# Layer 1 of a four-layer graph network: one joined product of turned h, and the splits, squares and bias moved around it

## The chip, the core and the metric

The kernel runs on one core of one Trainium2 chip. The time is device time in microseconds (us), the median of three runs. Engine names are those of the profile: PE (TensorE, matmuls; PEld are its weight loads), DVE (VectorE), ACT (ScalarE), POOL (GpSimd) and SP (SyncE, which here issues the DMAs). L12 means line 12 of the kernel.

## The reference, cut to what matters

x is 32 batches of 512 nodes with 128 features, adj is 512 x 512. Four graph layers follow each other; each adds its result to x. Layer 1 is the one that is changed:

```python
h = maximum(layernorm(x), 0)
x1 = einsum('bnf,nw->bwf', h, adj)             # first hop
x2 = 2 * einsum('bnf,nw->bwf', x1, adj) - h    # second hop
xs = stack([h, x1, x2, x1, x2])                # the two adjacencies of the layer are the same
x = x + relu(xs.reshape(b, n, 5 * 128) @ Theta1 + bias)
```

With Theta1 in five blocks of 128 rows, the kernel forms T0 = block 0 - (block 2 + block 4), T1 = block 1 + block 3 and T2 = 2 (block 2 + block 4), and computes `h T0 + adj^T (h T1 + x1 T2) + bias`: the own product h T0, the weighed product in the bracket, and one mix with adj for both hops. Layer 2 multiplies by the elementwise square of adj (`adj * adj`), which is why that square is prepared while layer 1 runs.

## The kernel before, in words

**Stages.** In the profiled execution layer 0 fills the time up to about 183 us, layer 1 runs from there to 450 us, layer 2 to about 645 us and layer 3 to the end. `tc.manual_schedule` makes PE, DVE, ACT and POOL run their instructions in the order in which the source writes them. SP's queue is ordered by the scheduler, except for DMAs under `keep_in_program_order`.

**Precision by parts.** Most large products run in F32R, a form of f32 that TensorE takes in one record, on three parts of each operand, `high`, `low` and `mid`: three F32R products accumulate into one PSUM bank. A product of plain f32 shows as two records. The parts of adj (`adj_parts`) are made once, at the end of layer 0. `moving_parts(x, high, low, mid)` splits a tile of 128 x 512: ACT writes high (L420), POOL low (L421), DVE mid (L422). `mixed_parts` is the product of such parts with `adj_parts`: twelve F32R matmuls with 512 columns (L405), and one ACT copy out (L407).

**Layer 1** works in rounds. A pair q holds two batches, b = 0 and 1; round r holds pairs A = 2r and C = 2r + 1, so there are 16 pairs and 8 rounds. For each pair:

- `normalised(q)`: eight ACT instructions make h (L285).
- `split_up(q, b)`: the three parts of h, node-major (`high_h`, `low_h`, `mid_h`).
- `turn(q)`: h turned to feature-major: two DVE transposes in blocks of 32 (L321), four DMA writes of the blocks to DRAM and one DMA load back as hT (L328, L330).
- `straighten(q)`: two POOL copies (L974) of hT into `hs`, in node order.
- `first(q, b)`: x1, feature-major, by `mixed_parts` of the parts of h.
- `weighed(q, b)`: for each of four blocks of 128 nodes, `hs T1 + x1 T2` as two plain f32 matmuls with 128 columns (L447), one PSUM bank in all; then w's three parts, high on ACT (L992), low and mid on DVE (L993, L994).

And for each round, `mix(r, i)` for the four node blocks i: first the own product `hs T0` as four plain f32 matmuls (L999), then twelve F32R matmuls of w's parts with `adj_parts` into the same bank (L1003), then two DVE passes: scale and bias (L1005), relu and the sum into x (L1007).

Round r writes its instructions so that the mixes of round r - 1 stand at its head: the PE order is mix(r-1, 0..3), first(A, 1), weighed(A, 0), weighed(A, 1), first(C, 0), first(C, 1), weighed(C, 0), weighed(C, 1), first(A+2, 0). Between them the source calls the splits, turns and normalisations of later pairs, `ln_stats` (layer norm statistics: four DVE instructions L245, a square root on ACT, two small DVE ones) for layer 2, and steps of `square`, the generator that makes the squared adjacency on POOL: it loads adj in crossed order, then for each of four blocks makes `sq_high` and `sq_low` in two steps (L1345 to L1349), and at the end `sq_mid` in four POOL instructions (L1354). `go(steps, n)` runs n steps of a generator. In the last round `more(k)` starts layer 2: its first h (`chunk`), their turning (`turn_half`, `fetch`) and the first two `features`. `messages(n)` is the first matmul group of layer 2: parts of the features with `sq_high`, `sq_low`, `sq_mid`.

**Buffers.** Tiles of 128 x 512 with the tag `small` (the parts of h, x1) share 13 buffers, the wide ones (parts of w and of the square) 6, `hT` and `hs` together 4, h 3. PSUM has 8 banks.

Of the kernel before, what the change touches and what calls it, by code (L numbers as in the profile page):

```python
# [9 lines left out]
F32 = mybir.dt.float32  # L10
# [19 lines left out]
def kernel(  # L30
# [369 lines left out]
    def mixed_parts(name, left, right, dst):  # L400
# [6 lines left out]
        nc.scalar.activation(dst, p, AF.Copy, scale=UP)  # L407
# [10 lines left out]
    def moving_parts(x, high, low, mid):  # L418

        nc.scalar.activation(high, x, AF.Copy, scale=DOWN)  # L420
        nc.gpsimd.tensor_sub(low, x, high.bitcast(F32))  # L421
        nc.vector.scalar_tensor_tensor(mid, x, 1.0 / UP, high.bitcast(F32), OP.mult, OP.subtract)  # L422

# [309 lines left out]
    def late_parts():  # L733
# [10 lines left out]
        nc.gpsimd.tensor_scalar(th[:, 0, :], th[:, 0, :], 1.0 / UP, None, OP.mult)  # L744
# [205 lines left out]
    def layer1(more, square):  # L950


        h, hT, hs, parts, x1, w = {}, {}, {}, {}, {}, {}
# [26 lines left out]

        def first(q, b):
# [4 lines left out]
        def weighed(q, b):  # L986
            r, j = q // 2, 2 * (q % 2) + b
            if j == 0:
                w[r] = [wide_tile(f"w_{part}_{r}", F32R) for part in PARTS]
            p = projected(f"p_w_{q}_{b}", (columns(hs[q][:, b]), th[:, 1, :]), (columns(x1[q, b]), th[:, 2, :]))  # L990
            high, low, mid = (part.rearrange("p t (w f) -> p t w f", f=D)[:, :, j, :] for part in w[r])
            nc.scalar.activation(high, p, AF.Copy, scale=DOWN)  # L992
            nc.vector.tensor_sub(low, p, high.bitcast(F32))  # L993
            nc.vector.scalar_tensor_tensor(mid, p, 1.0 / UP, high.bitcast(F32), OP.mult, OP.subtract)  # L994

        def mix(r, i):
            p = bank(f"p_l1_{r}_{i}")
            for j in range(4):
                nc.tensor.matmul(p[:, blk(j)], columns(hs[2 * r + j // 2][:, j % 2])(i), th[:, 0, :],  # L999
                                 start=(j == 0), stop=False, skip_group_check=True)  # L1000
            for part in range(3):
                for t in range(NT):
                    nc.tensor.matmul(p, adj_parts[part][:, t, blk(i)], w[r][part][:, t, :],  # L1003
                                     start=False, stop=(part == 2 and t == NT - 1), skip_group_check=True)
            nc.vector.scalar_tensor_tensor(tiles(p), tiles(p), UP, spread(b1, 4), OP.mult, OP.add)  # L1005
# [8 lines left out]
        split_up(0, 0)  # L1014
        split_up(0, 1)
        first(0, 0)
        straighten(0)
        turn(1)
        for r in range(NQ // 2):
            A, C = 2 * r, 2 * r + 1  # L1020
            last = r == NQ // 2 - 1
            if r == 0:
                first(A, 1)
                split_up(C, 0)
                split_up(C, 1)
                straighten(C)
            else:
# [5 lines left out]
                mix(r - 1, 1)  # L1033
                normalised(C)
                turn(C)
# [394 lines left out]
```

## Time and profile before

| | |
|---|---|
| median of 3 runs | 912.63 us (912.6 to 913.73) |
| profiled execution, own time | 912.96 us |
| its span, first to last instruction | 911.2 us |
| granted TensorE clock | 1.00 throughout |
| stretch of layer 1 in the trace | about 183.6 to 450.6 us |
| one round of layer 1 | 33.0 to 33.1 us |
| chain that ended last | PE 92%, ACT 3%, DVE 3%, POOL 1% |

The span is what the profile can be divided into; the own time of the same execution is 1.8 us longer, because it includes what lies before the first and after the last instruction. Busy shares on the page are means over four different layers, so a stage has to be read from its own stretch of the trace. Durations of matmul records overlap: two records of 275 ns can start 112 ns apart.

### The profile page before, as it was taken

How to read it: one execution, taken by the hardware profiler on the slowest of the kernel's cores; microseconds unless marked ns; L12 is line 12 of the kernel's file. 1: busy time of each engine (PE TensorE's matmuls, PEld its weight loads, DVE VectorE, ACT ScalarE, POOL GpSimd, SP SyncE). 2: the span in 40 equal slices, each digit the busy share in tenths (PEclk: the TensorE clock that was granted, in tenths of full speed). 3: DMA queues.
4: the chain of work that ended last, by engine and by line, in shares of the span. 5: the costliest groups of instructions: out<-in, count | busy, mean ns of one | idle time of the engine just before them, and what ended most of it. 6: DMA issues, size and time to landing. Idle time of an engine off the chain costs nothing.

```text
span 911.2 us, 15170 instructions
## 1 busy us (share of the span) xinstructions
PE 901.1 (99%) x5432; PEld 774.2 (85%) x5433; DVE 669.7 (74%) x1348; ACT 527.5 (58%) x1156; POOL 485.6 (53%) x435
## 2 busy tenths in 40 slices
PE   8999999999999999999999999999999999999998
PEld 4899999988888888888877777777789999999998
DVE  7888886566656665665767777777698888987775
ACT  5874554343532442452556768876577767666663
POOL 5867999932132163342254445545475555666553
PEclk9999999999999999999999999999999999999999
DMA  9255644123114313212332344455212223222111
GB/s 265 50 167 165 186 122 118 24 71 93 35 59 119 87 31 90 71 46 76 106 120 70 93 126 129 132 147 160 70 48 82 81 82 91 73 70 81 59 36 47
DMA packets 83915, 86.06 MB, mean 94 GB/s; under 512 B 6784, under 2 KB 74624, under 8 KB 83840
## 3 DMA queue, kind: packets, MB, share of 16 engines
q1 hardware_dynamic: 83552, 84.57, 32.8%
q8 instruction: 43, 0.70, 0.3%
q10 hardware_dynamic: 288, 0.52, 0.2%
q14 instruction: 32, 0.26, 0.1%
HBM read 44.17 MB, written 40.89 MB: 93 GB/s over the span
## 4 chain that ended last, share of the span: by engine, by line
PE 92%; ACT 3%; DVE 3%; POOL 1%; issue 0%; DMA 0%; DVEq 0%; POOLq 0%; ACTq 0%
PE p_av L1234 12%; PE p_l L1003 10%; PE p_x1T L405 9%; PE p_score L1212 9%; PE p_msgT L1142 9%; PE p_w L447 6%; PE p_l_c L393 4%; PE p_l L999 3%; PE p_l_a L393 3%; PE p_l_d L393 3%; PE p_g L447 3%; PE p_l L447 3%; PE p_hv L447 3%; PE p_feat L447 3%; PE p_phi L1151 3%; PE p_phi L1152 3%
## 5 line engine op out<-in xcount | busy, mean ns | idle before, releaser
L1234 PEld LDWEIGHTS p_av<-hv,ex 128*128 128x128 f32 x1024 | 119.3, 191 | 3.7 <-POOL ex L1207 1.0
L1234 PE MATMUL p_av<-hv,ex 128*128 128x129 f32 x1024 | 119.8, 274 | 0.8 <-POOL ex L1207 0.8
L421 POOL TENSOR_TENSOR low_feat<-feat,high_feat 128x512 fp32r<-128x512 f32 x32 | 53.9, 1686 | 115.8 <-ACT high_feat L420 111.7
L285 ACT ACTIVATE h<-x,sh,rs 128x128 f32<-128x128 f32 x256 | 102.8, 483 | 11.8 <-DVE sh L257 11.0
L1207 DVE TENSOR_TENSOR ex<-ex,adjTx 128x512 f32<-128x512 f32 x64 | 80.4, 1259 | 35.7 <-ACT ex L1205 34.0
L1207 POOL TENSOR_TENSOR ex<-ex,adjTx 128x512 f32<-128x512 f32 x64 | 98.1, 1551 | 12.2 <-ACT ex L1205 8.1
L1093 ACT ACTIVATE h<-x,sh,rs 128x128 f32<-128x128 f32 x256 | 102.9, 485 | 0.0
L428 POOL TENSOR_TENSOR key<-key 128x512 fp32r<-128x512 f32 x32 | 50.2, 1567 | 97.9 <-DVE key L427 39.8
L421 POOL TENSOR_TENSOR low_h<-h,high_h 128x512 fp32r<-128x512 f32 x32 | 47.1, 1482 | 76.6 <-ACT high_h L420 76.4
L245 DVE BATCH_NORM_STATS2 bn<-x 128x6 f32<-128x256 f32 x244 | 85.9, 417 | 0.0
L407 ACT ACTIVATE x1T<-p_x1T 128x512 f32<-128x512 f32 x32 | 19.0, 594 | 109.4 <-PE p_x1T L405 100.8
L1205 ACT ACTIVATE ex<-ex 128x512 f32<-128x512 f32 x128 | 78.9, 651 | 0.0
L1213 ACT ACTIVATE ex<-p_score 128x512 f32<-128x512 f32 x128 | 74.0, 604 | 1.4 <-PE p_score L1212 1.1
L974 POOL COPY hs<-hT 128x512 f32<-128x512 f32 x32 | 18.6, 612 | 81.5 <-DMA hT<-d_hT 81.3
L432 ACT ACTIVATE high_query<-p_query 128x512 fp32r<-128x512 f32 x32 | 19.2, 599 | 73.8 <-PE p_query L1185 73.8
L422 DVE SCALAR_TENSOR_TENSOR mid_feat<-feat,high_feat 128x512 fp32r<-128x512 f32 x32 | 28.9, 904 | 44.3 <-ACT high_feat L420 44.3
L1212 PE MATMUL p_score<-high_query,key 128*128 128x512 f32 x128 | 50.5, 394 | 0.0
L1212 PE MATMUL p_score<-low_query,key 128*128 128x512 f32 x128 | 50.3, 393 | 0.0
L1212 PE MATMUL p_score<-mid_query,key 128*128 128x512 f32 x128 | 50.3, 393 | 0.0
L447 PE MATMUL p_w<-th,x1T 128*128 128x128 f32 x256 | 49.6, 275 | 0.3 <-ACT x1T L407 0.3
L254 ACT ACTIVATE sd<-bn,eps 128x8 f32<-128x8 f32 x46 | 13.9, 302 | 61.5 <-DVE bn L245 57.4
L447 PE MATMUL p_w<-th,hs 128*128 128x128 f32 x256 | 49.4, 275 | 0.0
(220 smaller groups left out, 2350.4 us busy)
## 6 DMA issues: line engine op xcount, KB each, us to landing
d<-hb SPq DMA_DIRECT2D x128, 128.0 KB, 2.5
hT<-d SPq DMA_DIRECT2D x32, 512.0 KB, 3.4
d_hT<-hb_hT SPq DMA_DIRECT2D x112, 128.0 KB, 2.4
hT<-d_hT SPq DMA_DIRECT2D x28, 512.0 KB, 3.3
x<-in_x_dram SPq DMA_DIRECT2D x32, 256.0 KB, 5.0
out_dram<-x SPq DMA_DIRECT2D x31, 256.0 KB, 2.3
adjT_d<-adj_squares SPq DMA_DIRECT2D x4, 256.0 KB
adj_crossed<-in_adj_dram SPq DMA_DIRECT2D x4, 256.0 KB
```

The lines of the kernel that those rows point to most:

```text
L245: nc.vector.bn_stats(st[:, k].rearrange("p e s -> p (e s)"), xt[q][:, b, t : t + 2, :].rearrange("p t f -> p f t"))
L285: nc.scalar.activation(h[:, b, t, :], xt[q][:, b, t, :], AF.Relu, bias=shift[q][:, i : i + 1], scale=scale[q][:, i : i + 1])
L393: nc.tensor.matmul(p[:, i * 2 * D : (i + 1) * 2 * D], a[:, k, blk(i)], b[:, k], start=(first and i == 0 and k == 0), stop=(k == 1), skip_g ...
L405: nc.tensor.matmul(p, right[part][:, blk(t)], left[part][:, t, :], start=(t == 0 and part == 0), stop=(t == NT - 1 and part == 2))
L421: nc.gpsimd.tensor_sub(low, x, high.bitcast(F32))
L447: nc.tensor.matmul(p[:, blk(t)], hT(t), w, start=(i == 0), stop=(i == len(terms) - 1))
L1003: nc.tensor.matmul(p, adj_parts[part][:, t, blk(i)], w[r][part][:, t, :], start=False, stop=(part == 2 and t == NT - 1), skip_group_check= ...
L1093: nc.scalar.activation(h[:, t, :], xt[q][:, b, t, :], AF.Relu, bias=shift[q][:, i : i + 1], scale=scale[q][:, i : i + 1])
L1142: nc.tensor.matmul(p, feats[n][part][:, blk(t)], sq[part][:, t, :], start=(t == 0 and part == 0), stop=(t == NT - 1 and part == 2))
L1207: eng.tensor_mul(split(ex[:, t, :]), split(ex[:, t, :]), crossed(mask[:, t, :]))
L1212: nc.tensor.matmul(p, keys[n][i][:, t, :], query[n][i], start=(i == 0), stop=(i == 2))
L1234: nc.tensor.matmul(po[:, i, : D + 1], ex[:, t, blk(i0 + i)], hv[:, t, :], start=(t == 0), stop=(t == NT - 1))
```

## The change

- Turned h (`hs`) is split into three F32R parts as well (`split_turned`, new), and T0 and T1, which lie side by side in `th`, into three parts once (`fixed_parts`, new, 128 x 256).
- `weighed` multiplies the parts of turned h with T0 and T1 joined, 256 columns at once, so one product gives both the own product and the first term of the weighed one. x1 T2 stays a plain f32 matmul with 128 columns, added into the right half. A batch now fills two banks in place of one. Each bank is read by two ACT instructions (w's high part, and the own half, which is written over `hs`) and two DVE instructions (low, mid), each over half a bank.
- `biased_own` (new) adds the bias to the own half on POOL.
- `mix` loses its four f32 matmuls. Its first DVE pass becomes two half passes that add the own half; the second pass is unchanged.
- The factor `UP` moves from x1's copy and th into the evictions of `weighed`.
- The calls are written in a new order: at the entry three first products stand ahead of the first weighed one; in a round `split_up` of C moves behind the mixes and the new splits are spread between the products; `normalised` and `turn` of A + 2 move; the steps of `square` are called behind the third mix of rounds 3 to 6, two at a time; the statistics for layer 2 come two rounds later, and those of two more pairs fall into layer 2.

```diff
--- before.py
+++ after.py
@@ -404,7 +404,7 @@
             for t in range(NT):
                 nc.tensor.matmul(p, right[part][:, blk(t)], left[part][:, t, :],
                                  start=(t == 0 and part == 0), stop=(t == NT - 1 and part == 2))
-        nc.scalar.activation(dst, p, AF.Copy, scale=UP)
+        nc.scalar.copy(dst, p)
 
     def three(name):
         return [small_tile(f"{part}_{name}", F32R) for part in PARTS]
@@ -420,6 +420,13 @@
         nc.scalar.activation(high, x, AF.Copy, scale=DOWN)
         nc.gpsimd.tensor_sub(low, x, high.bitcast(F32))
         nc.vector.scalar_tensor_tensor(mid, x, 1.0 / UP, high.bitcast(F32), OP.mult, OP.subtract)
+
+    def fixed_parts(x, high, low, mid):
+
+        nc.scalar.activation(high, x, AF.Copy, scale=DOWN)
+        nc.gpsimd.tensor_sub(x, x, high.bitcast(F32))
+        nc.scalar.activation(low, x, AF.Copy, scale=LOW)
+        nc.gpsimd.tensor_sub(mid, high.bitcast(F32), low.bitcast(F32))
 
     def scaled_parts(x_low, high, low, mid):
 
@@ -741,7 +748,6 @@
         for out, op, p, q in ((1, OP.add, 1, 3), (2, OP.add, 2, 4), (0, OP.subtract, 0, 2)):
             tc.keep_in_program_order(nc.gpsimd.tensor_tensor(th[:, out, :], th[:, p, :], th[:, q, :], op))
         tc.keep_in_program_order(nc.gpsimd.tensor_scalar(th[:, 2, :], th[:, 2, :], 2.0, None, OP.mult))
-        nc.gpsimd.tensor_scalar(th[:, 0, :], th[:, 0, :], 1.0 / UP, None, OP.mult)
         for t in range(NT):
             nc.scalar.activation(low[:, t, :], adj_s[:, t, :], AF.Copy, scale=LOW)
         yield
@@ -950,7 +956,7 @@
     def layer1(more, square):
 
 
-        h, hT, hs, parts, x1, w = {}, {}, {}, {}, {}, {}
+        h, hT, hs, parts, hs_parts, x1, w = {}, {}, {}, {}, {}, {}, {}
         normal, turning = {}, {}
 
         def normalised(q, n=2 * NT):
@@ -978,31 +984,51 @@
                 parts[q, b] = three(f"h_{q}_{b}")
                 moving_parts(h[q][:, b].rearrange("p t f -> p (t f)"), *parts[q, b])
 
+        def split_turned(q, b):
+            hs_parts[q, b] = three(f"hs_{q}_{b}")
+            moving_parts(hs[q][:, b], *hs_parts[q, b])
+
         def first(q, b):
             if q < NQ:
                 x1[q, b] = small_tile(f"x1T_{q}_{b}")
                 mixed_parts(f"x1T_{q}_{b}", adj_parts, parts[q, b], x1[q, b])
 
         def weighed(q, b):
+
+
             r, j = q // 2, 2 * (q % 2) + b
             if j == 0:
                 w[r] = [wide_tile(f"w_{part}_{r}", F32R) for part in PARTS]
-            p = projected(f"p_w_{q}_{b}", (columns(hs[q][:, b]), th[:, 1, :]), (columns(x1[q, b]), th[:, 2, :]))
-            high, low, mid = (part.rearrange("p t (w f) -> p t w f", f=D)[:, :, j, :] for part in w[r])
-            nc.scalar.activation(high, p, AF.Copy, scale=DOWN)
-            nc.vector.tensor_sub(low, p, high.bitcast(F32))
-            nc.vector.scalar_tensor_tensor(mid, p, 1.0 / UP, high.bitcast(F32), OP.mult, OP.subtract)
+            ps = [bank(f"p_w_{q}_{b}_{i}") for i in range(2)]
+            for t in range(NT):
+                p = ps[t // 2][:, t % 2 * 2 * D : (t % 2 + 1) * 2 * D]
+                for part in range(3):
+                    nc.tensor.matmul(p, hs_parts[q, b][part][:, blk(t)], th_parts[part],
+                                     start=(part == 0 and t % 2 == 0), stop=False, skip_group_check=True)
+                nc.tensor.matmul(p[:, D:], x1[q, b][:, blk(t)], th[:, 2, :], start=False, stop=True,
+                                 skip_group_check=True)
+            for i, p in enumerate(ps):
+                p = p.rearrange("p (t k f) -> p k t f", t=2, k=2)
+                high, low, mid = (part.rearrange("p t (w f) -> p t w f", f=D)[:, 2 * i : 2 * i + 2, j, :]
+                                  for part in w[r])
+                nc.scalar.activation(high, p[:, 1], AF.Copy, scale=UP * DOWN)
+                nc.scalar.activation(tiles(hs[q][:, b])[:, 2 * i : 2 * i + 2, :], p[:, 0], AF.Copy, scale=UP)
+                nc.vector.scalar_tensor_tensor(low, p[:, 1], UP, high.bitcast(F32), OP.mult, OP.subtract)
+                nc.vector.tensor_sub(mid, p[:, 1], high.bitcast(F32))
+
+        def biased_own(q):
+            for b in range(2):
+                nc.gpsimd.tensor_add(tiles(hs[q][:, b]), tiles(hs[q][:, b]), spread(b1, NT))
 
         def mix(r, i):
             p = bank(f"p_l1_{r}_{i}")
-            for j in range(4):
-                nc.tensor.matmul(p[:, blk(j)], columns(hs[2 * r + j // 2][:, j % 2])(i), th[:, 0, :],
-                                 start=(j == 0), stop=False, skip_group_check=True)
             for part in range(3):
                 for t in range(NT):
                     nc.tensor.matmul(p, adj_parts[part][:, t, blk(i)], w[r][part][:, t, :],
-                                     start=False, stop=(part == 2 and t == NT - 1), skip_group_check=True)
-            nc.vector.scalar_tensor_tensor(tiles(p), tiles(p), UP, spread(b1, 4), OP.mult, OP.add)
+                                     start=(part == 0 and t == 0), stop=(part == 2 and t == NT - 1))
+            for k in range(2):
+                pk = tiles(p)[:, 2 * k : 2 * k + 2, :]
+                nc.vector.scalar_tensor_tensor(pk, pk, UP, hs[2 * r + k][:, :, blk(i)], OP.mult, OP.add)
             x = xq[r].rearrange("p w b t f -> p (w b) t f")[:, :, i, :]
             nc.vector.scalar_tensor_tensor(x, tiles(p), 0.0, x, OP.max, OP.add)
 
@@ -1011,64 +1037,75 @@
         turn(0)
         normalised(1)
         yield
-        split_up(0, 0)
-        split_up(0, 1)
+        for q, b in ((0, 0), (0, 1), (1, 0)):
+            split_up(q, b)
+        pair = small_tile("th_high", F32R), small_tile("th_low", F32R)
+        th_parts = pair[0][:, : 2 * D], pair[0][:, 2 * D :], pair[1][:, : 2 * D]
+        fixed_parts(th[:, 0:2, :].rearrange("p k f -> p (k f)"), *th_parts)
+        normalised(2)
+        straighten(0)
         first(0, 0)
-        straighten(0)
         turn(1)
+        split_turned(0, 0)
+        first(0, 1)
+        split_turned(0, 1)
+        first(1, 0)
+        straighten(1)
         for r in range(NQ // 2):
             A, C = 2 * r, 2 * r + 1
             last = r == NQ // 2 - 1
-            if r == 0:
-                first(A, 1)
-                split_up(C, 0)
-                split_up(C, 1)
-                straighten(C)
-            else:
+            early, late_stats = ((stats_steps(q) if r > 1 else iter(())) for q in (A - 4, C - 4))
+            if r:
                 split_up(A, 1)
                 straighten(A)
                 mix(r - 1, 0)
                 normalised(C, NT)
                 turn(C, 1)
                 mix(r - 1, 1)
+                go(early, NT)
                 normalised(C)
                 turn(C)
+                split_turned(A, 0)
                 mix(r - 1, 2)
+                split_turned(A, 1)
+                go(square, 2 * (2 < r < 7))
+                go(early, 1)
+                normalised(A + 2)
+                mix(r - 1, 3)
+                go(early)
+                first(A, 1)
                 split_up(C, 0)
-                go(square, r > 3)
-                mix(r - 1, 3)
-                split_up(C, 1)
-                first(A, 1)
+                straighten(C)
             weighed(A, 0)
+            split_up(C, 1)
             weighed(A, 1)
             if last:
                 more(0)
-            go(square, r > 2)
-            first(C, 0)
-            normalised(A + 2, NT)
+            split_turned(C, 0)
+            biased_own(A)
+            first(C, 0 if r else 1)
+            go(late_stats, NT)
             if last:
                 more(1)
+            split_turned(C, 1)
+            turn(A + 2, 1)
             if r:
-                ln_stats(A - 2)
-            else:
-                go(own[NQ - 3])
-                go(own[NQ - 2])
-            first(C, 1)
+                first(C, 1)
+            go(late_stats, 1)
             if last:
                 more(2)
-            if r:
-                straighten(C)
             split_up(A + 2, 0)
-            normalised(A + 2)
-            go(square, r > 3)
+            turn(A + 2)
             weighed(C, 0)
             weighed(C, 1)
-            ln_stats(C - 2) if r else go(own[NQ - 1])
-            go(square, r > 3)
-            turn(A + 2)
+            go(late_stats)
+            biased_own(C)
+            go(square, r == 2)
             first(A + 2, 0)
             if r == 0:
                 normalised(C + 2, 0)
+                for q in (NQ - 3, NQ - 2, NQ - 1):
+                    go(own[q])
         more(3)
         for i in range(NT):
             mix(r, i)
@@ -1287,8 +1324,8 @@
                 fetch(2, 2)
             elif n % 2 and n + 5 < B:
                 fetch(2, n // 2 + 3)
-            if n in (2, 3):
-                ln_stats(NQ - 4 + n)
+            if n in (2, 3, 4, 5):
+                ln_stats(NQ - 6 + n)
             if n == 12:
                 weights_of_3()
             if n == 20:
```

`fixed_parts`, `split_turned` and `biased_own` are new and stand in the diff in full; `moving_parts`, `stats_steps` and `bank` are not changed.

## The prediction

> **What bounds the kernel now.** I read the page's busy shares first, then the stage of layer 1 (179 to 451 us) by stretches, then who waited for whom on PE, and last the chain and single instructions.
>
> ```profile
> PE 901.1 (99%) x5432; PEld 774.2 (85%) x5433; DVE 669.7 (74%) x1348; ACT 527.5 (58%) x1156; POOL 485.6 (53%) x435
> ...
> 352.50:385.50 33.00, 33.00 (x194) 28.73 (x193) 20.09 (x36) 13.29 (x30) 15.43 (x17) 1.00 0.24 65
> ...
> PE p_w L447 <- ACT x1T L407: 0.3, 1, 0.3
> ```
>
> The second line is one round of layer 1 (columns: stretch, its length, busy PE, PEld, DVE, ACT, POOL, granted clock, DMA share, GB/s): PE has no free moment in 33 us, the next engine is at 61%. The last is PE's only wait in the whole layer. So a round lasts as long as its matmuls, and the change has to be priced by how far apart matmuls start. A record overlaps the next one, so spacing comes from the chain:
>
> ```profile
> 388.34 3.57 PE p_w L447 x32
> ...
> 404.71 2.80 PE p_l L1003 x12
> 408.40 2.81 PE p_l L1003 x12
> ```
>
> 32 records of weighed in 3.57 us: an f32 product with 128 columns is two records of 111.6 ns, 223 ns in all. Twelve F32R products with 512 columns take 2.80 us, 233 ns each. One mix follows the other by 3.69 us, so its eight records of L999 (the own product) take 0.89 us.
>
> **What the Trainium skill says.** "TensorE: Matmul & The Clock Gate", Back-to-back issue gap and LDWEIGHTS: warm matmuls start N/2.4 + 2.5 ns apart, 128 weight columns load in 107 ns. For 512 bf16 columns the trace agrees (six in 1.29 us, 216 ns); the F32R products lie 17 ns above it, and no page prices F32R. Its section on the clock gate: about 3.4 us without matmuls halve the clock. PE's longest wait here is 2.0 us and the clock is 1.00 throughout, so no trace shows that. "SBUF — State Buffer", two separate sides: VectorE with two SBUF inputs and GpSimd exclude each other from a shared port pair. In the tile views mid_h on DVE takes 681 to 1761 ns and low_h on POOL 1272 to 1803 ns, which fits; I use both ends.
>
> **The change, part by part.**
>
> 1. *The product on PE.* Per batch it removes 16 f32 records in weighed and 8 in mix: 24 x 111.6 = 2.68 us. It adds 12 F32R products with 256 columns and keeps 8 f32 records for x1T (0.89 us). No row has the 256-column form. Weights:
>
> ```profile
> 371.37 0.30 PEld L1003 LDWEIGHTS p_l<-w_high,adj_high 128*128 128x128 f32 x2
> L1003 PEld LDWEIGHTS p_l<-w_low,adj_low 128*128 128x128 f32 x128 | 24.1, 188 | 5.9
> ```
>
> Two F32R loads in 0.30 us, each 188 ns long: the second starts 0.11 us after the first, so a load allows 112 to 116 ns. Streaming: half of 233 is 116 ns; if the 17 ns are a fixed charge it is 126 ns. I take 121 ns: 12 x 121 + 893 = 2.35 us, a gain of 0.334 us per batch, 32 times **-10.7 us** (116 ns: -12.6; 126 ns: -8.8). Switches between f32 and F32R: a mix takes 3.696 us against 8 x 111.6 + 12 x 232.7 = 3.685, so about 5.5 ns each. Four more per batch: **+0.7**.
>
> 2. *What the other engines get, per round.* ACT: four high parts (0.60) and 16 evictions of half a bank (0.37, the ACT row L342) for four of 0.59: +5.9, 19.2 us. DVE: four mid parts at 0.98, 16 half evictions at 0.42 (DVE row L342) for eight at 0.69, half a pass more per mix: about +5.7, 25.8 us. POOL: four low parts at 1.48, four bias adds at 1.28 (as L841): +11, 19.4 us, 23 where it squares. A round of PE is then 31.8 us, so none becomes the bound by load.
>
> 3. *Order inside a round.* PE, from the first mix: mixes to 11.2; first(A,1) 14.0; weighed(A) 16.3 and 18.7; first(C) 21.5 and 24.3; weighed(C,0) 26.6; weighed(C,1) 29.0; first(A+2,0) 31.8. The new wait is weighed's for the parts of turned h. The tight one is (C,1): ACT splits (C,0) behind the last eviction of weighed(A,1), at 20.1; then POOL does low(C,0) 1.3, two bias adds 2.6, low(C,1) 1.3, done at 25.3, needed at 26.7. Slack 1.4 us. Turned h of C: transposed by 9.5, and at the entry the transposes' end (177.9) to the copy (186.1) takes 8.1, so it is there at 17.6; straighten and low_h(C,1) end at 20.1, just ahead of that chain. Behind it on POOL wait low_h(A+2,0) and bias C, both with over 2 us. SP keeps its instructions; each pair's four writes are now followed by its own load, while before some loads sat behind the other pair's write. The half-bank evictions use two banks a batch; sixteen banks a round are two turns of eight and each is read in time. Small tiles: 13, less two for th's parts; the count reaches 11 behind x1 of (A,1), and every later split stands in ACT's queue behind a copy that already waited for the release. Cost **+0.4**; ends 0 and 8.
>
> 4. *Entry.* Three first products (8.4 us) stand ahead of weighed(0,0). In that time POOL has low(1,0), two pieces of th (0.77 each, as L1169) and straighten(0) ahead of low(0,0); ACT has eight normalisations (3.1 us) ahead of high(0,0). Low(0,0) ends at 192.5 against 192.1. Later turned h of pair 1 lands near 196 and holds low_h(1,1): 0.7; in round 0 only one first product lies between weighed(0,1) and weighed(1,0), so low(1,1), behind two bias adds, is 1.0 late. 2.1 less the 0.3 there now: **+1.8**; ends 0 and 4.
>
> 5. *The square's mid part.* Two steps a round from rounds 3 to 6 complete high and low. The mid part falls to the call after layer 1, on POOL behind low_feat of batch 1; before, it was made at 387 us.
>
> ```profile
> L1354 POOL TENSOR_TENSOR sq_mid<-sq_high,sq_low x4: 1260/1273/1717, 387.4 to 391.6; 128x512 fp32r<-128x512 f32 x4
> ...
> 449.67 1.77 POOL L421 TENSOR_TENSOR low_feat<-feat,high_feat 128x512 fp32r<-128x512 f32 x1 [2.27 <-ACT high_feat L420]
> ...
> 450.74 2.77 PE p_msgT L1142 x12
> ```
>
> Counted from the end of the second mix, low_feat of batch 1 ends at 9.9 now and about 10.2 after (DVE's mix is a little longer); PE reaches messages(0) at 0.89 + 2.8 + 0.89 + 2.8 = 7.4, and its mid products at 9.2. The four pieces come at 11.5, 12.7, 14.0 and 15.2; PE ends at 15.5 for 10.2. **+5.3**; ends 3 and 8, the latter if the clock is halved for a while. What queues behind is messages(1) and features(2), whose parts are ready by then.
>
> 6. *At nothing.* Plain copies for scaled ones and th's scale dropped: same instructions, one POOL piece less, under layer 0's matmuls. Statistics of four pairs move from layer 1 into blocks 2 to 5 of layer 2, 1.8 us on DVE each; DVE has 1.8 us free in a block of 6.3 and blocks 2 and 3 carry it already. If that cover goes, 1 us. The last round's work for layer 2 lies on ACT ahead of high(C,1), inside the slack of 3.
>
> Sum: -10.7 + 0.7 + 0.4 + 1.8 + 5.3 = **-2.5 us**. The profiled execution took 912.96 us (span 911.2), 0.3 over the median of 912.63, so 910.5 there and 910.2 against the median. 0.2% is 1.8 us, what a measurement can tell from no change.
>
> **Rivals.**
>
> *The waits shrink (0.15).* The product at 116 ns and an entry without waits: -12.6 + 0.7 + 5.3 = -6.6, 906. For it: PE's present lack of any wait; against it: item 5's queue order, which is fixed.
>
> *POOL sets the round (0.25), slower.* The place is low(C,1) behind the bias adds. With low parts at 1.8 and adds at 1.5 the chain ends at 26.7 and the slack is gone; each further 0.1 us is lost in seven rounds. Being 1 us late costs 7 us: +4.5, 917; at 1.4 us 920. It decides from about 0.6 us. For it: low_feat's 1.77 us on a POOL that meets DVE; against it: low_h's median of 1304 ns.
>
> *256 columns give no gain (0.05), slower.* If the F32R product stays at 233 ns whatever its width, weighed takes 3.69 us a batch: +32 us, 942. The load spacing speaks against it. Outside my range.
>
> **Numbers.** Main case 0.55, its own range 906 to 914: of it 0.33 faster, 0.17 same, 0.05 slower. With the rivals: faster 0.49, same 0.21, slower 0.30. The range 903 to 918 takes in the cheap product with few waits and POOL about 1 us late a round.
>
> **What would show it.** Right: L1006 products 116 to 126 ns apart; rounds of about 32 us with PE full; a wait of PE for sq_mid near 5 us at the first messages. Wrong: weighed waiting for low_hs in every round; L1006 spaced by more than 149 ns, where item 1's gain is gone; no wait for sq_mid.

## The result and the profile after

The kernel after takes **920.34 us** (median of four runs, 920.09 to 921.09) against 912.82 before (912.60 to 913.73): 1.0082 of the time before, 95% interval 1.0064 to 1.0099. It is slower by 7.5 us where the prediction said 910.2, range 903 to 918. The profiled execution has a span of 918.5 us, 7.3 over the 911.2 before.

First the page's busy row, then PE's waits (engine, line, waited for: us in total, times, longest):

```profile
PE 897.3 (98%) x5304; PEld 765.6 (83%) x5305; DVE 709.0 (77%) x1476; ACT 569.4 (62%) x1286; POOL 583.8 (64%) x500
```

```profile
PE p_w L1006 <- POOL low_hs L421: 6.8, 5, 2.0
PE p_msgT L1179 <- POOL sq_mid L1391: 3.6, 4, 2.2
```

PE is recorded busy for 3.8 us less and still ends later. Before, its only wait in layer 1 was 0.3 us; now there are five stops of `weighed` for the low part of turned h, 6.8 us, and four at the first messages, 3.6 us. A view of stretches and a piece of the chain show that the product itself is as fast as hoped:

```profile
343.90:375.50 31.60, 31.60 (x178) 27.28 (x177) 25.66 (x52) 18.40 (x46) 24.33 (x20) 1.00 0.24 68
```

```profile
421.67 0.36 PE p_w L1006 x3
422.03 0.22 PE p_w L1008 x2
422.25 0.36 PE p_w L1006 x3
```

In an undisturbed round PE is full (31.60 of 31.60 us) and the round lasts 31.6 us where it lasted 33.05; three products with 256 columns take 0.36 us, 120 ns each. The next line of stretches is round 3 of the same kernel: 34.02 us long, PE busy 32.15.

```profile
278.18:312.20 34.02, 32.15 (x177) 27.29 (x177) 25.71 (x52) 18.61 (x46) 23.66 (x20) 1.00 0.33 101
```

The starts of landmarks in the two timelines (first product of x1T, first mix of round 0, first mix of round 7, first product of messages(0), of messages(2), end) split the 7.3 us. The same table for all kernels that ran is used below; a stage in it is from one profiled execution each, the time is the median of the runs.

| kernel | time | to layer 1 | entry | first mix of round 0 to that of round 7 | last mixes | messages 0, 1 | rest |
|---|---|---|---|---|---|---|---|
| before | 912.8 | 183.6 | 21.7 | 228.7 | 16.7 | 8.7 | 452.0 |
| **after** | **920.3** | 184.5 | 29.5 | 222.9 | 13.4 | 15.6 | 452.7 |
| sq_early | 913.1 | 183.5 | 29.5 | 224.5 | 13.4 | 8.7 | 453.4 |
| bias_late | 914.3 | 185.2 | 27.2 | 219.4 | 13.4 | 16.2 | 452.4 |
| norm_late | 919.7 | 184.9 | 26.6 | 224.8 | 13.4 | 16.6 | 452.4 |
| all_three | 906.9 | 183.7 | 27.0 | 219.3 | 13.4 | 8.7 | 453.0 |
| load_early | 916.6 | 184.2 | 28.0 | 220.7 | 13.3 | 16.5 | 452.5 |
| idle_fill | 919.6 | 184.4 | 27.9 | 223.5 | 13.4 | 14.3 | 453.6 |
| product_back | 917.7 | 183.5 | 23.8 | 228.8 | 16.6 | 8.6 | 454.4 |
| old_sq_late | 917.7 | 183.5 | 21.7 | 228.6 | 16.6 | 13.7 | 451.7 |
| best | 903.4 | 185.1 | 24.6 | 218.3 | 13.4 | 8.7 | 453.0 |
| best_stats | 903.9 | 183.7 | 24.6 | 218.3 | 13.4 | 8.7 | 453.4 |

(In the entry, 2.1 us of the difference to before is own product that now lies in `weighed` instead of in the mixes. The column before it differs by 1.7 us between kernels whose code is the same there: chance. In sq_early and norm_late the fourth column contains a fall of the clock in round 3, about 1.5 us, and in product_back the last column contains one in layer 2.)

**The entry.** PE's timeline of after, with the idle time before each instruction and its releaser in brackets, and POOL's just before the second stop:

```profile
194.84 0.39 PE L1006 MATMUL p_w<-th_high,low_hs 128*128 128x256 f32 x1 [1.47 <-POOL low_hs L421]
...
207.30 0.39 PE L1006 MATMUL p_w<-th_high,low_hs 128*128 128x256 f32 x1 [2.04 <-POOL low_hs L421]
```

```profile
202.16 3.42 POOL L1021 TENSOR_TENSOR hs<-hs,b 128x512 f32<-128x512 f32 x2
205.53 1.72 POOL L421 TENSOR_TENSOR low_hs<-hs,high_hs 128x512 fp32r<-128x512 f32 x1
```

At the first stop POOL itself had waited, 2.24 us for the high part from ACT, which stood behind the eight normalisations of pair 2; then the low part took 1.73 us. At the second, the low part of (1,1) stands behind two bias adds, which take 3.42 us, and itself takes 1.72. The stretch that follows has a clock of 0.72:

```profile
207.00:210.70 3.70, 3.40 (x20) 3.40 (x21) 1.81 (x6) 0.67 (x3) 2.73 (x3) 0.72 0.56 142
```

**The first messages.** PE's timeline, then two stretches:

```profile
454.44 0.80 PE L1179 MATMUL p_msgT<-sq_mid,mid_feat 128*128 128x512 f32 x1 [2.25 <-POOL sq_mid L1391]
455.67 0.79 PE L1179 MATMUL p_msgT<-sq_mid,mid_feat 128*128 128x512 f32 x1 [0.44 <-POOL sq_mid L1391]
456.90 0.79 PE L1179 MATMUL p_msgT<-sq_mid,mid_feat 128*128 128x512 f32 x1 [0.43 <-POOL sq_mid L1391]
458.12 0.79 PE L1179 MATMUL p_msgT<-sq_mid,mid_feat 128*128 128x512 f32 x1 [0.43 <-POOL sq_mid L1391]
458.72 1.91 PE L454 MATMUL p_feat<-psi,hT 128*128 128x128 f32 x8
```

```profile
452.00:455.00 3.00, 0.75 (x2) 0.29 (x1) 2.93 (x7) 3.00 (x9) 3.00 (x3) 0.89 0.01 3
455.00:458.20 3.20, 1.89 (x4) 0.65 (x3) 0.37 (x1) 0.92 (x3) 3.20 (x4) 0.50 0.64 164
```

POOL delivers a piece of sq_mid every 1.23 us, and PE takes one at a time, at half clock: a product is recorded with 0.79 us where it has 0.39 elsewhere, and the eight of p_feat behind them still with 1.91 us, where before they had 1.05. The recorded idle of 3.6 us is too small a figure for the loss: the slow products hide part of the wait. Without a stop the four products would have ended 2.8 us after the start of messages(0), as before; they end 8.2 after it (458.12 plus about 0.25, from 450.15). So the wait is 5.4 us, and the other 1.5 of this stage's 7.0 is the low clock.

**Round 3.** SP's and POOL's timelines of after:

```profile
279.23 2.66 SPq L116 DMA_DIRECT2D adj_crossed<-in_adj_dram  x4
287.44 1.76 SPq L328 DMA_DIRECT2D d_hT<-hb_hT  x4
294.86 0.34 SPq L330 DMA_DIRECT2D hT<-d_hT  x1
```

```profile
298.15 1.17 POOL L980 COPY hs<-hT 128x512 f32<-128x512 f32 x2 [2.96 <-DMA hT<-d_hT]
...
302.25 2.97 POOL L1021 TENSOR_TENSOR hs<-hs,b 128x512 f32<-128x512 f32 x2
305.18 1.72 POOL L421 TENSOR_TENSOR low_hs<-hs,high_hs 128x512 fp32r<-128x512 f32 x1
```

The load of adjacency for the square is still moving when pair 7's four writes are issued (100 GB/s between 285.5 and 287.4 us; in load_early, below, nothing moves in the two microseconds ahead of these writes); these let the load behind them start 7.4 us later (294.86 - 287.44). POOL waits 2.96 us for hT, and then the bias adds come ahead of the low part that PE waits for.

So the product's gain of about 11.8 us (eight rounds, each 1.48 us shorter when undisturbed) was all there, and about 19 us went elsewhere. The experiments ask whether these are the causes, and what each is worth.

### The profile page after: what moved, and what is told of

Its sections match the earlier page's. It is cut to its first block, busy times and chain, and to the rows that moved or that the text cites. A ratio compares the mean times of both kernels' runs of the same rounds, so it can differ in the third digit from the quotient of the medians.

```text
span 918.5 us, 15433 instructions
## 1 busy us (share of the span) xinstructions
PE 897.3 (98%) x5304; PEld 765.6 (83%) x5305; DVE 709.0 (77%) x1476; ACT 569.4 (62%) x1286; POOL 583.8 (64%) x500
## 4 chain that ended last, share of the span: by engine, by line
PE 84%; DVE 6%; ACT 4%; POOL 3%; DMA 1%; issue 1%; SPq 0%; DVEq 0%; POOLq 0%; ACTq 0%
PE p_av L1271 12%; PE p_l L1027 9%; PE p_score L1249 9%; PE p_x1T L405 8%; PE p_msgT L1179 7%; PE p_w L1006 5%; PE p_l_c L393 4%; PE p_w L1008 3%; PE p_l_d L393 3%; PE p_hv L454 3%; PE p_g L454 3%; PE p_l_a L393 3%; PE p_l L454 3%; PE p_feat L454 2%; PE p_query L1222 2%; PE p_phi L1188 2%
## 5 line engine op out<-in xcount | busy, mean ns | idle before, releaser
L421 POOL TENSOR_TENSOR low_feat<-feat,high_feat 128x512 fp32r<-128x512 f32 x32 | 56.1, 1753 | 102.8 <-ACT high_feat L420 102.8
L285 ACT ACTIVATE h<-x,sh,rs 128x128 f32<-128x128 f32 x256 | 102.2, 483 | 12.8 <-DVE sh L257 11.8
L421 POOL TENSOR_TENSOR low_h<-h,high_h 128x512 fp32r<-128x512 f32 x32 | 51.9, 1622 | 53.5 <-ACT high_h L420 27.2
L439 ACT ACTIVATE high_query<-p_query 128x512 fp32r<-128x512 f32 x32 | 19.2, 600 | 74.0 <-PE p_query L1222 74.0
L422 DVE SCALAR_TENSOR_TENSOR mid_feat<-feat,high_feat 128x512 fp32r<-128x512 f32 x32 | 24.4, 763 | 44.3 <-ACT high_feat L420 44.3
L421 POOL TENSOR_TENSOR low_hs<-hs,high_hs 128x512 fp32r<-128x512 f32 x32 | 46.6, 1466 | 8.9 <-ACT high_hs L420 7.1
L407 ACT COPY x1T<-p_x1T 128x512 f32<-128x512 f32 x32 | 18.7, 585 | 52.1 <-PE p_x1T L405 51.9
L1021 POOL TENSOR_TENSOR hs<-hs,b 128x512 f32<-128x512 f32 x32 | 45.0, 1414 | 8.5 <-PE p_w L1008 6.0
```

The lines of the kernel that those rows point to most:

```text
L285: nc.scalar.activation(h[:, b, t, :], xt[q][:, b, t, :], AF.Relu, bias=shift[q][:, i : i + 1], scale=scale[q][:, i : i + 1])
```

## The experiments

**Three edits one by one, and together.** Each takes away one cause.

sq_early, the mid part in round 7, behind the last bias adds:

```diff
-            go(square, r == 2)
+            go(square, r in (2, 7))
```

> One step moved: the square's mid part is made behind the last bias adds of round 7, some 13 us ahead of messages(0), instead of in the call after layer 1. Theory (the wait for sq_mid and the halved clock behind it are the +7.1 us seen between the first messages product and the third): 920.3 - 7.1 = about 913.2, the clock 1.00 in this stage, no wait for sq_mid. Rival 1 (the clock fell for another reason and only the recorded waits of 3.6 us go): 916.7. Rival 2 (the stage is held by the statistics of pairs 12 to 15, now all in layer 2): 920, with a wait for DVE in the place of the one for POOL.

Measured 913.07 us (1.0002 of before, 0.9994 to 1.0011). The wait is gone, the stage lasts 8.7 us again, no other wait takes its place. Theory held: 7.3 us, twice the recorded idle of 3.6. Its fourteen runs spread from 910.8 to 915.5, more than before's; in the profiled one round 3 took 35.5 us, 1.5 more than in after with the same stop of 1.77 us, because the clock fell to 0.50 behind it (306.62 to 310.03). The spread follows the clock: the four runs with a mean granted clock of 0.999 or 1.000 have a median of 911.7, the six with 0.997 or 0.998 one of 913.1, the four with 0.996 one of 914.8. A stretch of 3.4 us at half clock takes 0.002 off the mean, so each cost about 1.5 us, and without any this kernel is about 1 us below before.

bias_late, in every round:

```diff
             split_turned(C, 0)
-            biased_own(A)
...
             split_turned(C, 1)
+            biased_own(A)
```

> One line moved: the two bias adds of pair A stand behind the low part of turned h of (C,1) instead of ahead of it, in all eight rounds. Theory (these adds, 3.0 to 3.4 us on POOL, make low_hs of (C,1) late): the waits of weighed in rounds 1, 3 and 7 go (0.6 + 1.8 + 0.9, with what follows them some 4 us), at the entry the second stop of 2.0 us goes and about 1 us of the low clock: 913.5 to 914.5. Rival (POOL has too much to do in a round, so the wait only passes on to the next user, the mixes that need the biased own product or low_h of A + 2): 919 to 921, with waits for L1021 or low_h.

Measured 914.30 (1.0017, 1.0009 to 1.0024), 6.0 less than after and inside the theory's range. Rounds 1 and 7 are quiet (31.6 and, to the last mixes, 28.7 us), round 3 falls from 34.0 to 32.7, the second stop at the entry is gone. Part of the rival is true as well: the adds now stand ahead of low_h of pair 2, and `first` waits for it 0.8 us at the entry.

norm_late, the normalisations of pair 2 at the entry, in two halves:

```diff
-        normalised(2)
         straighten(0)
...
         straighten(1)
+        normalised(2, NT)
...
+            if r == 0:
+                normalised(2)
             first(C, 0 if r else 1)
```

> Entry only: the eight normalisations of pair 2 (3.2 us on ACT) stand behind the parts of turned h of pair 0, one half after straighten(1), the other after the bias adds of round 0. Theory (they make high_hs of (0,0) late, and with it low_hs and PE by 1.5 us): the first stop goes and with one stop less the clock holds longer: 920.3 - 1.5 - about 0.9 = 918. Rival (PE only comes sooner to the second stop, for low_hs of (1,1), which is set by POOL's queue): 920, second stop 3 us or more.

Measured 919.71 (1.0070, 1.0058 to 1.0082): 0.6 less than after, where the intervals overlap. The trace says more than the time. The first stop is gone, the second falls from 2.0 to 1.3 us, and the entry is 2.9 us shorter, about 1.5 of it because the clock held there; but `first` of (1,1) now waits 1.5 us for low_h, which had come in time behind the stop. In the profiled run round 3 took 36.0 us instead of 34.0: `first` waits 0.6 us for low_h there, and the clock fell (0.50 from 305.75 to 309.16). So a stop taken away alone is in part passed on, as the rival said, though the second stop of 3 us or more that it named did not come; and the two of the five runs with the least low clock (mean 0.996, the others 0.993 or 0.994) took 918.0 and 918.6 us, near the theory's 918.

> The three edits together: mid part of the square in round 7, bias adds behind the low parts, normalisations of pair 2 off the way. Theory (the new waits and the clock that falls in them are all that eats the product's gain): -7.1 at the first messages, about -4 in the rounds, -5 at the entry: 904 to 905, below both kernels. Rival (the waits share one cause, POOL's load, and pass on): the sum of the three single effects is not reached, 908 to 912.

Measured 906.85 (0.9932, 0.9919 to 0.9945). The three single effects add to 13.9 us, together they give 13.5. It misses the 904 to 905 of the theory by what is seen left over: PE waits 1.5 and 0.8 us for low_h and 0.6 for low_hs at the entry, and round 3 is 1.0 us over the quiet ones.

**Is the low clock a cost of its own?** idle_fill puts products that nobody reads into the wait for sq_mid:

```diff
+        idle = bank("p_idle_sq") if n == 0 else None
         for part in range(3):
             for t in range(NT):
+                for _ in range((4 if t else 10) * (n == 0 and part == 2)):
+                    nc.tensor.matmul(idle, feats[n][0][:, blk(t)], sq[0][:, t, :], start=True, stop=True)
```

> The changed kernel with 22 F32R products of 512 columns added, whose result nobody reads: ten ahead of the first product of messages(0) that needs sq_mid and four ahead of each of the next three, so that PE works through the wait instead of standing. The wait itself stays. Theory (the +7.1 us of this stage are a wait of 5.3, from where the first of these products could have started to where the fourth did, and 1.8 for the clock that falls in it): the clock stays at 1.00 and only the 1.8 go, 920.3 - 1.8 = 918.5. Rival 1 (the clock is the larger part; recorded idle is only 3.6): 916.8. Rival 2 (the clock falls for another reason than PE's standing): 920.3 or, with the added products in the way, 921.

The stretch of the wait in this kernel:

```profile
454.00:457.00 3.00, 3.00 (x14) 2.13 (x13) 0.41 (x1) 0.96 (x3) 3.00 (x3) 1.00 0.69 175
```

The clock is 1.00, and the stage lasts 14.3 us instead of 15.6: the fourth product ends 8.35 us after the start of messages(0), so the wait is the same 5.5, and what follows runs as fast as before. PE's standing is thereby shown to be the cause of the low clock in this stage. The time is 919.60 (1.0071, 1.0059 to 1.0084), only 0.7 less than after, and the intervals overlap: PE then waits 0.6 us for msgT on DVE, and the rest of the profiled run is 0.9 us longer. By time alone theory and second rival are not told apart; the price of the low clock rests on the stretches of the traces and on the fourteen runs of sq_early.

**Round 3.** load_early moves the load of adjacency into a pause of SP's queue:

```diff
             weighed(A, 1)
+            go(square, r == 2)
...
-            go(square, r == 2)
```

> The changed kernel with one step moved: the load of adjacency for its square (four transfers of 256 KB) is issued behind weighed(4,1), in the pause of SP's queue between the turned h of pair 5 and of pair 6, instead of at the end of round 2, where it runs into the four writes of pair 7. Theory (these writes take 8 us instead of 4 from issue to the load behind them, POOL then waits 3 us for turned h of pair 7 and round 3 lasts 34.0 instead of 31.6 us): round 3 falls to about 31.6, 920.3 - 2.4 = 917.9. Rival (the load disturbs whichever turn is nearest, or round 3 has another cause, the bias adds alone): 920, with the wait now in round 2 or still in round 3.

Measured 916.64 (1.0041, 1.0028 to 1.0054), 3.7 less than after. Round 3 lasts 31.6 us although the bias adds still stand ahead of the low part: the adds alone cost this round nothing, the late load alone costs 1.0 us (bias_late, 32.7), and both together 2.4. SP's timeline of this kernel shows the load of pair 7 issued 3.7 us after its writes:

```profile
285.79 1.76 SPq L328 DMA_DIRECT2D d_hT<-hb_hT  x4
289.53 0.34 SPq L330 DMA_DIRECT2D hT<-d_hT  x1
```

That is 2.4 of the 3.7 us. In the profiled executions the entry, whose code is unchanged, is 1.5 us shorter as well, and that is again the clock. The two stops of PE are the same (1.47 and 2.05 us by the timeline), but the stretch behind them shows, for this kernel:

```profile
207.00:210.70 3.70, 3.65 (x25) 3.43 (x26) 2.01 (x7) 1.32 (x4) 2.83 (x3) 1.00 0.56 142
```

With after's entry the clock fell in two kernels (after, sq_early: entry 29.5 us) and held in two (load_early, idle_fill: 28.0 and 27.9). So 1.5 us of the entry are a matter of chance from execution to execution; the rest is the stops. How much of the 3.7 us by the medians is this chance stays open: two of the five runs of load_early have after's mean clock of 0.994 and took 916.6 us all the same.

**How much is the product worth, and what does the order do without it?** product_back is all_three with the products of before:

```diff
-            ps = [bank(f"p_w_{q}_{b}_{i}") for i in range(2)]
...
+            p = projected(f"p_w_{q}_{b}", (columns(hs[q][:, b]), th[:, 1, :]), (columns(x1[q, b]), th[:, 2, :]))
...
         def mix(r, i):
             p = bank(f"p_l1_{r}_{i}")
+            for j in range(4):
+                nc.tensor.matmul(p[:, blk(j)], columns(hs[2 * r + j // 2][:, j % 2])(i), th[:, 0, :],
+                                 start=(j == 0), stop=False, skip_group_check=True)
```

> The version with the three edits (906.85), but with the products of before: weighed on 128 f32 columns, the own product in each mix, x1T and Theta scaled as before, no parts of turned h and no bias adds. The order of everything else stays. Theory (the product is worth 32 x 0.37 = 11.8 us on PE, less the waits for its parts that this version still has, about 1 in round 3 and 3 at the entry): 906.85 + 11.8 - 4 = 914.5, between 913 and 916.5. Rival (the new order is what gains, the product little): under 910.

Measured 917.66 (1.0050, 1.0037 to 1.0062): 10.8 us more than with the product, where 7.6 was expected. The direction of the theory held, its size not: I had counted the product's waits, but not that the order has waits without it too. At the entry PE waits 2.4 us for low_h of (1,1), which stands behind a late straighten(1). In layer 2 block 7 lasts 9.7 us, where before has 6.3 and all_three 8.1; what it is longer than in all_three is mostly the clock, which fell to 0.50 there (501.28 to 504.69). The mean clock was 0.997 or 0.998 in all five runs, 0.999 or 1.000 in those of all_three, so some 1.5 of the 10.8 us is the clock and not the product. The order of all_three without the product costs 4.7 us against before; it gains nothing by itself.

**The late mid part alone, in the old kernel.** old_sq_late is before with

```diff
+        yield from range(40)
         sq.append(wide_tile(f"sq_{PARTS[2]}", F32R))
```

> The kernel before, with one thing of the change alone: the square's mid part is put off to the call after layer 1 (forty empty steps ahead of it), everything else as it was. Theory (the late mid part costs what it costs whatever the product is: 5.3 of wait and 1.8 of low clock): 912.8 + 7.1 = 919.9, with a wait for sq_mid at the first messages and a clock of about 0.5 in it. Rival (in the old kernel POOL is less loaded, the four pieces follow low_feat sooner and the clock holds): 912.8 + 4 = 917.

Measured 917.68 (1.0059, 1.0047 to 1.0072), 5.0 more than before and not 7.1. Here the rival's 917 came close, and for a reason that could have been worked out: in the old kernel the last two mixes ahead of messages(0) contain own products of 0.89 us each, so PE arrives 1.8 us later beside the same chain of POOL. The four products end 6.1 us after the start of messages(0) (456.32 plus 0.25, from 450.47): a wait of 3.3, and 1.7 for the clock, which falls to 0.50 here as well. The one run of six with a mean clock of 1.000 took 916.35 us, 3.7 more than before: little but the wait. In the changed kernel the wait is 5.4. The product's gain in the last mixes is turned into wait.

**A version without these waits.** best has the three edits, the load moved as in load_early, and:

```diff
             split_turned(C, 1)
-            biased_own(A)
             turn(A + 2, 1)
...
+            biased_own(A)
             biased_own(C)
...
         split_up(0, 1)
+        turn(1)
         split_up(1, 0)
...
+        split_up(1, 1)
         normalised(2, NT)
         straighten(1)
```

> The three edits and three more: the load of adjacency moved as above; the bias adds of A directly ahead of those of C, so behind low_h of A + 2 too; at the entry the transposes of pair 1 ahead of the parts of h(1,0), and the parts of h(1,1) ahead of straighten(1). Theory (what is left over the quiet rounds are PE's waits for low_h and low_hs: 1.5 + 0.6 + 0.8 at the entry and 1.0 in round 3): 906.85 - 3.9 = 903. Rival (the entry is bound by POOL's total work, so the waits pass on): 905 to 906, with only round 3 better.

Measured **903.42** (0.9891, 0.9876 to 0.9906): 9.5 us below the 912.97 of before in the same comparison, 16.9 below after. Apart from the load, the further edits were not run singly. PE's waits in it for what were the culprits:

```profile
PE p_w L1006 <- POOL low_hs L421: 0.4, 2, 0.2
```

The first six intervals from mix to mix last 31.5 to 31.6 us, the seventh, up to the last mixes, 28.7, and the entry 24.6.

> The version with six edits, and the statistics of pairs 12 to 15 in blocks 2, 4, 6 and 8 of layer 2 instead of 2, 3, 4 and 5, so that none shares a block with the statistics that updated makes in every second block. Theory (the two of them in one block, 1.4 us each on DVE, are what makes block 2 last 7.1 instead of 6.6 and block 7 8.1 instead of 6.3): 903.4 - 1.0 to - 2.3, about 901.8. Rival (block 7 waits for something else, the parts of features or the chunk's normalisation on ACT): 903.4, block 7 still 8.1.

Its edit:

```diff
-            if n in (2, 3, 4, 5):
-                ln_stats(NQ - 6 + n)
+            if n in (2, 4, 6, 8):
+                ln_stats(NQ - 5 + n // 2)
```

Measured 903.90 (0.9904, 0.9889 to 0.9918), no change. Block 7 does fall to 6.3 us, but block 10 now takes 8.2 and block 11 7.3: the stop has moved to where the last statistics are. ACT's timeline there:

```profile
501.78 0.30 ACT L254 ACTIVATE sd<-bn,eps 128x8 f32<-128x8 f32 x1 [3.32 <-DVE bn L245]
501.99 3.18 ACT L1136 ACTIVATE h<-x,sh,rs 128x128 f32<-128x128 f32 x8
505.07 0.61 ACT L1174 ACTIVATE feat<-feat 128x512 f32<-128x512 f32 x1
505.71 0.63 ACT L420 ACTIVATE high_feat<-feat 128x512 fp32r<-128x512 f32 x1
506.25 0.67 ACT L1196 ACTIVATE msgT<-p_phi,phi1b 128x512 f32<-128x512 f32 x1
```

The square root of the statistics waits 3.3 us for DVE at the head of ACT's queue; behind it stand eight normalisations (from block 7 on each block has two chunks) and, at the end, the msgT that PE waits for, 1.5 us. So the two statistics in one block did hold block 7, but keeping them apart is not enough: with them in a later block the stop comes there. An earlier place, with all four ahead of block 5, was not tried.

## Why the prediction was wrong

The sign was wrong, although each mechanism in its sum is in the trace. What it costs beside the product's gain was sized at 7.5 us and came to about 19. The steps that failed are the slack of item 3 (+0.4 for what measured +4.7), the entry of item 4 (+1.8 for +5.7), and the low clock, which the main value left out at the entry and in item 5 (about 1.5 us each).

1. **The product** was right: -10.0 with the switches was predicted, and a quiet round is 1.48 us shorter (33.06 to 31.58, times eight: -11.8). The spacing of 119 to 120 ns is near the 121 taken; four blocks take 2.31 to 2.32 us, which leaves no room for the charge of 0.7 us for more switches. On the chip the product was worth 10.8 us in product_back, net of other waits and with one fall of the clock in it.
2. **Loads** were right in what they said: no engine fills a round. ACT was 18.4 us for 19.2 predicted, DVE 25.7 for 25.8, POOL 24.3 for 23. But loads say nothing of order, and all the loss is in order.
3. **Order inside a round** failed: +0.4 predicted, some +4.7 measured (rounds of 32.5 and 34.0 us, and 29.9 for a quiet 28.7 up to the last mixes). The step that failed is "Slack 1.4 us" of low(C,1) behind the bias adds. It was worked out with 1.3 us for an instruction of POOL; beside DVE the pair of adds took 3.0 and a low part up to 1.8. In quiet rounds the slack just holds. It fails where a second thing comes late: in round 3 the hT of pair 7, in round 7 the work for layer 2 on ACT, put down as "inside the slack of 3", in round 1 0.6 us. "SP keeps its instructions" overlooked that the load of adjacency had moved across the writes of a pair. The rival with POOL had the right place and about the right size for the rounds, and moving the adds gave 6.0 us back; its form, a little late in all rounds, was wrong. That it also names 920 for 1.4 us a round is luck: the rounds lost 4.7 us, and the rest of the 920.3 comes from the entry and the first messages.
4. **The entry** failed most: +1.8 predicted, +5.7 measured (7.8 less the 2.1 of moved product), outside its own ends of 0 to 4. Both stops had been found, with the right instructions ahead of them, but low(0,0) ended at 194.8 and not at 192.5, and low(1,1) was 2.0 late and not 1.0. For low(0,0) the queues of POOL and ACT stand one behind the other, where the prediction names them side by side: ACT's second piece of th waited 2.7 us for POOL's low(1,0) and first piece (1.73 us for 1.3, and 1.18 for 0.77), the eight normalisations came behind it, POOL then waited 2.24 us for high(0,0), and the low part took 1.73. For low(1,1) it was the durations, 3.42 for the adds taken as 2.6 and 1.72 for the low part. On top came 1.5 us for the clock, which was not in the sum.
5. **The square's mid part**: the wait was right (5.3 predicted, 5.4 measured), and so was its sentence on the upper end, "if the clock is halved for a while". It was; that is the other 1.5. The low clock should have been in the main value.
6. **At nothing**: the moved statistics are the likely cause of the 0.75 us that the rest of the program is longer (1.0 in best, where block 2 takes 7.1 us for 6.6 before and block 7 8.1 for 6.3; before had two such blocks further on, 13 and 15, of 7.2 and 7.3). The prediction had named the 1 us "if that cover goes". About another 0.8 us lies ahead of layer 1, where the code hardly changed, and is chance.

One sum among the rivals is off: 256 columns at 233 ns would have cost 32 us in the place of the gain of 10.7, so with the other terms about 953 and not 942.

What was said to show the prediction wrong, a wait for low_hs in every round, did not come: the waits were in four places, and that was enough. In each of items 3 to 5 the upper end lay nearer to the truth than the main value, in item 5 because of the clock, in items 3 and 4 largely because of POOL beside DVE. The prediction had both ends of these durations from the trace before and took the short one, though the change itself put more onto both engines. The Trainium skill ("SBUF — State Buffer", two separate sides) says that the two exclude each other from a port pair, the one that starts first keeping it; the mean of low_h on POOL rose from 1482 ns before to 1622 after, which fits, and the single durations, in the last section, agree in detail.

## What to carry to other kernels

A part that comes just in time is sized with the slow duration of its engine, above all when the change itself loads that engine and its neighbour; and a slack is spent by whatever else is late in that round, so it is checked in the first, the last and every round with an extra transfer. Work that frees PE ahead of a fixed chain on another engine only lengthens the wait behind it: what a later product needs has to move up with the gain. Of instructions on a queue with one reader waiting, those that nobody waits for go last; here two lines moved (the mid part, the bias adds) were worth 7.3 and 6.0 us, each alone. A difference of 1.5 us between two medians can be one fall of the clock more or less, so the mean clock of each run belongs beside its time.

## What the runs showed of the hardware

- **The clock falls in stops shorter than the window.** The Trainium skill ("TensorE: Matmul & The Clock Gate", Part 1: The HAM clock gate) gives a free-running window of about 3.4 us, and an idle one halves the clock. In each trace here all changes of the clock lie on one grid of 3.413 us, which fits a window that runs on freely; but no window had to be idle, and on this the measurements decide. The columns are as in the stretches above. The first two lines are two windows at the entry of after, the other two the same place in load_early:

```profile
205.19:208.60 3.41, 1.37 (x12) 1.30 (x12) 2.86 (x6) 0.65 (x2) 3.41 (x4) 1.00 0.25 58
208.60:212.01 3.41, 3.41 (x15) 3.12 (x14) 1.39 (x4) 1.32 (x4) 1.66 (x2) 0.50 0.51 127
203.25:206.66 3.41, 1.75 (x16) 1.55 (x14) 3.32 (x5) 1.83 (x6) 3.41 (x3) 1.00 0.02 5
206.66:210.07 3.41, 3.02 (x23) 2.89 (x24) 1.89 (x6) 1.18 (x4) 2.81 (x3) 1.00 0.61 154
```

In after the whole stop of 2.04 us lies in one window, PE is busy for 1.37 us of it, and the next window has half the clock. In load_early the same stop lies across two windows, 1.66 us of it in the first, and the clock holds; idle_fill is like load_early, sq_early like after. Of the 3120 windows of this grid that the twelve traces have between 10 and 905 us with the clock at 1.00, the twelve with the least recorded work of PE (0.15 to 1.65 us of 3.41) were followed by a fall, and none of the others. So here the limit is PE busy for a little under half of a window, as far as the profile's modelled ends of matmuls can tell. In old_sq_late a fall came with recorded stops of no more than 0.74 us, several in one window. Each fall at the entry and at the first messages cost 1.5 to 1.7 us beyond the wait.
- **POOL and DVE delay each other, and which of them starts first decides.** In layer 1 the 128 x 512 subtractions and additions on POOL (low parts, bias adds) take 1.26 to 1.32 us or 1.71 to 1.84, never anything between. In the twelve traces together, 528 of them are overlapped by exactly one mid instruction of DVE, which reads two tiles of SBUF. Where DVE had started first (351), all but one take the long time; where POOL had started first (177), all take the short one, and in 175 the DVE instruction is the longer, over 0.8 us for 0.68. Those that no mid instruction overlaps are all short. So these durations are not a spread but two cases: with the bias adds moved, as in best, all 32 are short. First after, then best (least, median and longest duration in ns):

```profile
L1021 POOL TENSOR_TENSOR hs<-hs,b x32: 1272/1290/1755, 202.2 to 437.9; 128x512 f32<-128x512 f32 x32
L1021 POOL TENSOR_TENSOR hs<-hs,b x32: 1269/1287/1302, 206.2 to 429.1; 128x512 f32<-128x512 f32 x32
```

- **An F32R product with 256 columns** starts 119 to 120 ns after the one ahead of it, about half of the 233 ns with 512 columns, with a new load of weights each time.
- **One megabyte in the wrong gap.** Four transfers of 256 KB, issued 8 us ahead of a pair's four writes, made these writes hold back the load behind them by 7.4 us instead of 3.7.
